# A DiT block in float32: conditioning matmuls placed between two transposes, an elementwise division on another engine, and the last transposes and stores interleaved

## The chip, the cores and the metric

The kernel runs on one core of one Trainium2 chip. The metric is the device time of one launch in microseconds (us). The engines are named as the profile names them: PE (TensorE, matmuls and transposes), PEld (its weight loads), DVE (VectorE), ACT (ScalarE), POOL (GpSimd) and SP (SyncE, which issues most DMAs).

## The reference

Input x is 2 × 2048 × 512 (batch, token, channel), cond is 2 × 512. There are 16 heads of 32 channels; the MLP is 2048 wide.

```python
mod = silu(condition) @ Wada + bada                      # 512 -> 6 x 512
sh_a, sc_a, gt_a, sh_m, sc_m, gt_m = split(mod, 6)
xn = layernorm(x, g1, be1)
xm = xn * (1 + sc_a) + sh_a
x  = x + gt_a * causal_attention(xm, Wqkv, Wproj, bproj)
xn = layernorm(x, g2, be2)
xm = xn * (1 + sc_m) + sh_m
h  = gelu(xm @ W1 + b1)                                  # exact gelu
x  = x + gt_m * (h @ W2 + b2)
```

Everything is float32. In the profile a 128x128 by 128x512 float32 matmul appears as two instructions, so a call of `mm` on such operands counts x2.

## The kernel before

**Stages.** The work goes through the core in this order (times from the trace): startup to about 20 us (first x rows, layer norm statistics, the first two conditioning columns, transposes); q, k and v of batch 0 (to about 215 us), with attention scores woven in between; attention of batch 0 (to 761.8); its projection (`project_phase`, to 820.7); the same for batch 1 (projection 1552.2 to 1611.8); the MLP in four blocks `m` of 1024 tokens, written as a Strassen product with 7 instead of 8 block products (1611.8 to 2415.8); the last block's rows are transposed back and stored (to 2423.1).

**What sets the order.** `mm`, `transpose` and `act` put an instruction into program order on its engine; other DVE, ACT and POOL instructions are placed by a scheduler, which respects data and buffers. DMAs are issued in order by the engine that they are written for (`nc.sync` is SP, `nc.scalar` ACT, `nc.gpsimd` POOL). PSUM has eight banks: six in the pool of the matmuls of the stage (tag `mm`), and two in a pool with tag `s`, which the attention scores (`s`), `ps_mod` and `ps_modt` of the conditioning share; in the MLP these two are a pool of their own for `ps_o`.

**Startup.** `transposed` (L224 on) normalizes x tiles of 128 tokens on DVE (`xn`, L238), transposes them on PE into `ps_xt` (L208) and returns `modulate`, which scales and shifts the four channel chunks into `xmT`, even chunks on DVE (L257), odd ones on ACT (L262). A group of 512 tokens has two halves j = 0, 1 (`norm(g, j)`). `modulation(s0)` computes two of the six column groups: 8 calls of `mm` into `ps_mod` from `w` (the `wada` tile, 2 MB in eight loads), the bias added by DVE (`mr`, L1065), 4 small `mm` that turn rows into columns (`ps_modt`), and a copy (`mod`, L1074). `scale_shift` makes `a` and `c` from them. `picks` makes two constants, `pickc` (4 columns, used by `ps_modt`) and `pick` (L131, 128x512, first used in attention). The order is: stats, both halves' transposes, `picks`, `modulation(0)`, `scale_shift`, both `modulate`, q/k/v.

**q, k and v.** For each of four groups g of 512 tokens, `group` runs products n = 0 to 7 (q and k of four heads each, `ps_qk`) and n = 8 to 11 (v). `among` weaves score matmuls of earlier groups between the matmuls for g > 0; DVE takes each score bank's maxima (`mx`, L455), which frees the bank. After products 5 and 8 the next group's halves are normalized and transposed. After product 3, `modulation(2)` runs in g = 1 and `modulation(3)` in g = 2, the latter followed by `scale_shift`.

**Projection.** `project_phase` takes 16 tiles of 128 tokens, in four chunks k of four tiles. A tile is 4 calls of `mm` into `ps_o`. Attention's outputs arrive undivided: `at` (and at k = 1 a tile that the trace names `kst`) holds 512 tokens × 512 channels of them, `rbs` (the trace's `qst`) the inverse sums spread to the same shape. While chunk k runs, `d` of chunk k + 1 is multiplied by `rbs` (L996), one 128x512 operation for each tile, twelve in a batch. Beside it POOL adds the projection's bias to x for k > 0 (L983), DVE adds x to `ps_o` (L990) and makes the layer norm statistics of the result (L212, L215). For chunk 0 both the division and POOL's addition (L428) are done before the phase. In the first projection, `between` also normalizes and transposes batch 1's first group (n = 5 and 8), and issues the load of Wqkv from POOL at n = 6.

**MLP tail.** For each m, `tail` makes seven products (n = 0 to 6, `ps_y`) with two output chunks each (dd = 0, 1), eight calls of `mm` (f = 0 to 7). Product 6 completes `yt[dd][0]` in `p7`: DVE subtracts (`combine`), ACT scales and shifts (`done`, L1342). `rows_out` transposes `yt` back (PE, `ps_o`, L208), DVE adds the residual (L1410), and SP stores 128 tokens × 512 channels (L1414). In the last m, the rows of group 1 (all four chunks) go ahead of the matmul f = 4 of product 6, dd = 0; chunks 0, 2 and 3 of group 0 go ahead of f = 4 of dd = 1; chunk 1 of group 0 follows after the last product, with the stores of group 0.

Of the kernel before, what the change touches and what calls it, by code (L numbers as in the profile page):

```python
# [17 lines left out]
P = 128  # L18
# [9 lines left out]
def dit_block_kernel(  # L28
# [99 lines left out]
    def picks():  # L128
        two = ident.rearrange("p (k r b) -> p k r b", k=2, r=2)[:, :, :, :B]
        nc.vector.tensor_tensor(pickc, two[:, 0], two[:, 1], ALU.add)  # L130
        nc.vector.tensor_copy(pick, pickc.unsqueeze(3).to_broadcast([P, 2, B, P]))  # L131


    first = const.tile([P, 1], F32, tag="first", name="first")
# [63 lines left out]
    def mm(*args, **kw):  # L198

        return tc.keep_in_program_order(nc.tensor.matmul(*args, **kw))  # L200

    def act(ins):

        return tc.keep_in_program_order(ins)
# [22 lines left out]
    def transposed(pool_, psum, xts, n0, mv, rstd, a, c, b, dst):  # L227

        count = len(xts)
        per = 512 // (count * P)
        xns = []
        for t, xt in enumerate(xts):
            xn = pool_.tile([P, D], F32, tag="xn", name="xn", bufs=3)
            n = n0 + t
            nc.vector.tensor_scalar(  # L238
                xn, xt, mv[:, n, 0:1], rstd[:, n : n + 1], ALU.subtract, ALU.mult
            )  # L240
# [12 lines left out]
        def modulate():  # L253
            for k in range(C):
                src = banks[k // per][:, k % per, :]
                if k % 2 == 0:
                    nc.vector.tensor_scalar(  # L257
                        dst[:, k, :], src,
                        a[:, k, b : b + 1], c[:, k, b : b + 1], ALU.mult, ALU.add,
                    )  # L260
# [679 lines left out]
    def project_phase(row, psum, between):  # L940

        b = row.b
        with pool(f"proj{b}") as pp:
            n = 0
            ats = list(row.at_s)
            rbs = {1: row.rb_s[1], 2: row.old_queries(), 3: row.rb_s[0]}
            rows_x = [b * NT + i * TQ + t for i in last_order for t in range(TQ)]  # L950
            xts = list(row.xt_s)

            def tokens(upto):
                while len(xts) < min(upto, NT):
                    xt = pp.tile([P, D], F32, tag="xt", name="xt", bufs=6)
                    nc.sync.dma_start(xt, x_rows(rows_x[len(xts)]))
                    xts.append(xt)

            row.load_sums(len(units) - 1, len(units))
            tokens(TQ + 6)  # L960
            for k, i in enumerate(last_order):
                if k in (0, 1):

                    at = pp.tile([P, C, QB], F32, tag="at", name="at", bufs=2)
                    nc.sync.dma_start(at, od[b][last_order[k + 2]])
                    ats.append(at)
                at = ats[k]
                for t in range(TQ):

                    if n == 0:  # L970
                        nc.sync.dma_start(rbs[2], wide_d[b][last_order[2]])
                        nc.sync.dma_start(
                            rbs[3][:, : C - 1], wide_d[b][last_order[3]][:, : C - 1]
                        )
                    elif n == 3:
                        row.invert(len(units) - 1, len(units))
                    elif n == 4:
                        row.widen(len(units) - 1, rbs[3][:, C - 1, :])

                    tokens(n + 6)  # L980
                    nt, xt = rows_x[n], xts[n]
                    if k > 0:
                        act(nc.gpsimd.tensor_tensor(xt, xt, bgate, ALU.add))  # L983
                    ps = psum.tile([P, D], F32, tag="mm", name="ps_o")
                    for c in range(C):
                        mm(
                            ps, at[:, c, t * P : (t + 1) * P], row.wproj[:, c, :],
                            start=(c == 0), stop=(c == C - 1),
                        )
                    nc.vector.tensor_tensor(xt, ps, xt, ALU.add)  # L990
                    stats(pp, xt, nt, mv2, True)
                    nc.sync.dma_start(x1d[nt], xt)
                    if k + 1 < NQ:
                        d = ats[k + 1][:, t, :]
                        act(
                            nc.vector.tensor_tensor(d, d, rbs[k + 1][:, t, :], ALU.mult)  # L996
                        )
                    between(n)
                    n += 1
        inv_std(mv2, rstd2, b * NT, (b + 1) * NT)  # L1000
# [3 lines left out]
    with pool("wada") as wp, pool("qkv0") as qp, pool(  # L1004
# [44 lines left out]
        def modulation(s0):  # L1049

            w, mr = wada.pop(s0)
            ps = ps_sp.tile([P, D], F32, tag="s", name="ps_mod")
            for k in range(C // 2):
                for half in range(2):
                    for n in range(2):
                        at = (2 * half + n) * HD
                        kk = half * C // 2 + k  # L1060
                        mm(
                            ps[at : at + HD, :], sc[:, kk, :], w[:, n, kk, :],
                            start=(k == 0), stop=(k == C // 2 - 1),
                        )
            nc.vector.tensor_tensor(mr, ps, mr, ALU.add)  # L1065
            if s0 % 3 == 2:
                return
            ps_t = ps_sp.tile([P, C, 2, B], F32, tag="s", name="ps_modt")
            for k in range(C):
                mm(  # L1070
                    ps_t[:, k], mr[:, k * P : (k + 1) * P], pickc,
                    start=True, stop=True,
                )
            nc.vector.tensor_copy(mod[:, s0 : s0 + 2], ps_t.rearrange("p c s b -> p s c b"))  # L1074

        def scale_shift(a, c, r_g, r_be, shift, scale):

# [7 lines left out]

        for t in range(MTT):
            qkv.stats(0, t)
        halves = [qkv.norm(0, j) for j in range(2)]

        act(  # L1090
            nc.scalar.activation(
# [1 line left out]
            )  # L1093
        )
        picks()
        modulation(0)
        scale_shift(a1, c1, r_g1, r_be1, 0, 1)
        for modulate in halves:
            modulate()

        def also(g, n):

            if g == NG - 1 and n % 2 == 0:
                quarters.step()
            if g == 0 and n == 2:
                load_wada(2, 5)
            elif g == 1 and n == 3:
                modulation(2)
                load_wada(3, 4)
            elif g == 2 and n == 3:  # L1110
                modulation(3)
                scale_shift(a2, c2, r_g2, r_be2, 3, 4)

        quarters = Quarters()
        with pool("hl0") as hp:
# [52 lines left out]
    with ExitStack() as mlp:  # L1168
# [75 lines left out]
        def combine(dst, x, y, op):  # L1244
            nc.vector.tensor_tensor(dst, x, y, op)  # L1245
# [44 lines left out]
        def tail(m, h, yt, w2s, between, among):  # L1290
# [47 lines left out]
                    tiles.append(t)  # L1338
                return lambda f: tiles[f // 2][:, f % 2, :]

            def done(chunk, g):
                nc.scalar.activation(  # L1342
                    yt[chunk][g], yt[chunk][g], AF.Identity,
                    bias=gbias[:, chunk, b : b + 1], scale=gb[:, chunk, b : b + 1],
                )

# [26 lines left out]
                done(HK + dd, 1)  # L1373

            def p7(dd, ps):
                combine(yt[dd][0], us[dd], ps, ALU.subtract)
                done(dd, 0)


            b11, b12, b21, b22 = (0, 0), (1, 0), (0, 1), (1, 1)  # L1380
# [16 lines left out]
                xts.append(xt)  # L1397
            return xts

        def rows_out(m, yt, g, xts, parts, last):  # L1400

            for t in range(MTT):
                ps = ps_op.tile([P, D], F32, tag="o", name="ps_o")
                for lo, hi in parts:
                    for k in range(lo, hi):
# [5 lines left out]
                if last:  # L1411
                    n = (2 * m + g) * MTT + t
                    t0 = (n % NT) * P
                    nc.sync.dma_start(out[n // NT, t0 : t0 + P, :], xts[t])  # L1414

        ready = None
        for m in range(NM):
# [42 lines left out]
            else:  # L1460
# [4 lines left out]

                def among(n, dd, f):

                    if n == 6 and f == HF // 2:
                        if dd == 0:
                            rows_out(m, yt, 1, res[1], [(0, C)], True)  # L1470
                        else:
                            rows_out(m, yt, 0, res[0], [(0, 1), (HK, C)], False)

            tail(m, h, yt, w2s, between, among)
            ready = yt
# [36 lines left out]
```

## Time and profile before

| | us |
|---|---|
| median of 3 runs (lowest, highest) | 2423.33 (2420.83, 2425.81) |
| the profiled execution, its time | 2424.88 |
| its span in the trace | 2423.1 |
| PE busy | 2388.1 (99%) |
| DVE busy | 1358.6 (56%) |
| POOL busy | 1096.5 (45%) |
| ACT busy | 895.1 (37%) |
| mean granted PE clock | 0.997 of full speed |

The profile of one execution was read. Times count from the span's start. A line such as `L996 DVE TENSOR_TENSOR at<-at,qst 128x512 ... x8 | 5.3, 662 | 0.0` says: line 996, engine, operation, output and inputs by their names, shape, number of instructions, busy time in us, mean ns of one, and the idle time of the engine before them, with what ended it. The chain of waits follows the last instruction back to what released it, step by step. The table by stretch gives each engine's busy time in a stretch, the clock that PE was granted (1.00 or 0.50 here), the mean busy share of the DMA engines and their GB/s. Some matmul records are missing from the trace (a block of 8 transposes shows x7).

### The profile page before, as it was taken

Reading aid. Unit: us, or ns where it says so; the run is one execution under the profiler, and the core shown is the slowest. Engines: PE = TensorE matmul, PEld = TensorE weight load, DVE = VectorE, ACT = ScalarE, POOL = GpSimd, SP = SyncE. Lnnn points to the kernel's source line nnn. Section 1 sums busy time; section 2 is a strip of 40 time slices with the busy share of each in tenths; the row PEclk is TensorE's granted clock in tenths of the full one; section 3 lists DMA queues with packets and bytes.
Section 4 is the critical chain, followed back from the end, with each engine's and each line's share of the span. In section 5 each row is a group of like instructions: output and inputs, shape, how many; then the busy total and the mean of one; then the engine's idle time right before and its main releaser. Section 6 shows DMA issues by size and latency. Waiting matters only on the chain.

```text
span 2423.1 us, 31009 instructions
## 1 busy us (share of the span) xinstructions
PE 2388.1 (99%) x10797; PEld 1169.3 (48%) x10797; DVE 1358.6 (56%) x2836; ACT 895.1 (37%) x1670; POOL 1096.5 (45%) x1255
## 2 busy tenths in 40 slices
PE   8999999999999999999999999999999999999998
PEld 3455555555544445555555554444444444444443
DVE  3466666767657536676676765773344263353424
ACT  2213555555554121255555555423213213312310
POOL 1062998978773451199797878322001101100200
PEclk9999999999999999999999999999999999999999
DMA  7677215051325794621515132452324233223323
GB/s 244 195 236 192 53 34 110 23 114 45 105 98 193 216 323 157 158 56 33 120 25 114 45 100 89 166 180 76 110 77 146 76 111 130 80 91 99 114 82 100
DMA packets 132853, 285.72 MB, mean 118 GB/s; under 512 B 13472, under 2 KB 42700, under 8 KB 127832
## 3 DMA queue, kind: packets, MB, share of 16 engines
q1 hardware_dynamic: 126224, 257.46, 35.9%
q0 software_dynamic: 6384, 26.25, 3.1%
q8 instruction: 85, 1.39, 0.2%
q14 instruction: 72, 0.59, 0.1%
q10 hardware_dynamic: 88, 0.02, 0.0%
HBM read 209.76 MB, written 81.79 MB: 120 GB/s over the span
## 4 chain that ended last, share of the span: by engine, by line
PE 95%; DVE 3%; POOL 1%; DMA 1%; issue 1%; ACT 0%; SPq 0%; DVEq 0%; POOLq 0%; ACTq 0%
PE st L200 19%; PE ps_y L200 16%; PE ps_h L200 16%; PE o L200 11%; PE s L200 10%; PE ps_qk L200 8%; PE ps_v L200 4%; PE ps_o L200 4%; PE sm L200 4%; PE ps_xt L208 1%; POOL ee L608 1%; DMA x<-in_x_dram 1%; PE ps_o L208 0%; DVE junk L450 0%; DVE mx L455 0%
## 5 line engine op out<-in xcount | busy, mean ns | idle before, releaser
L580 ACT ACTIVATE e<-st 128x512 f32<-128x512 f32 (+1 forms) x1152 | 573.5, 578 | 427.9 <-PE st L200 363.0
L608 POOL TENSOR_TENSOR ee<-ee,e 128x512 f32<-128x512 f32 x424 | 529.3, 1289 | 4.5 <-ACT e L580 4.2
L455 DVE TENSOR_REDUCE mx<-s 128x1 f32<-128x512 f32 x604 | 407.7, 687 | 205.4 <-PE s L200 204.3
L200 PE MATMUL s<-kst,qst 128*128 128x512 f32 (+3 forms) x1032 | 465.0, 452 | 5.2 <-DVE mx L455 3.2
L200 PE MATMUL st<-qst,kst 128*128 128x512 f32 (+3 forms) x1280 | 409.4, 387 | 0.0
L1283 POOL TENSOR_TENSOR c<-c 128x512 f32<-128x512 f32 x32 | 40.7, 1273 | 625.6 <-DVE c L1245 562.8
L200 PE MATMUL o<-e,vv 128*32 128x512 f32 (+3 forms) x2560 | 300.4, 538 | 2.0 <-POOL e L586 2.0
L200 PE MATMUL ps_h<-sx,w 128*128 128x512 f32 x640 | 286.7, 592 | 0.0
L450 DVE CUSTOM_DVE_ANT_0 junk<-s,causal 128x512 bf16<-128x512 f32 (+3 forms) x428 | 209.1, 488 | 134.0 <-PE s L200 125.7
L200 PE MATMUL ps_y<-sh,w 128*128 128x512 f32 x640 | 278.3, 595 | 0.0
L200 PEld LDWEIGHTS st<-qst,kst 128*128 128x128 f32 x1280 | 227.4, 188 | 94.2 <-issue 62.1
L200 PEld LDWEIGHTS s<-kst,qst 128*128 128x128 f32 x1032 | 194.8, 189 | 155.4 <-DVE mx L455 53.8
L608 POOL TENSOR_TENSOR ee<-e 128x512 f32<-128x512 f32 x168 | 210.4, 1286 | 101.0 <-ACT e L580 100.6
L200 PE MATMUL ps_qk<-xmT,wqkv 128*128 128x512 f32 x512 | 242.8, 602 | 2.2 <-DVE xmT L257 2.2
L1245 DVE TENSOR_TENSOR h<-c,ps_h 128x512 f32<-128x512 f32 x128 | 88.1, 688 | 232.5 <-PE ps_h L200 232.5
L586 POOL TENSOR_SCALAR_AFFINE_SELECT e<-e 128x128 f32<-128x128 f32 (+1 forms) x384 | 122.2, 356 | 200.5 <-ACT e L580 197.8
L200 PEld LDWEIGHTS ps_h<-sx,w 128*128 128x128 f32 x640 | 121.1, 190 | 150.2 <-issue 149.5
L200 PEld LDWEIGHTS ps_y<-sh,w 128*128 128x128 f32 x640 | 121.3, 191 | 148.9 <-issue 147.5
L1269 ACT ACTIVATE h<-h,cols 128x512 f32<-128x512 f32 x128 | 92.4, 722 | 182.0 <-DVE h L1245 182.0
L200 PE MATMUL st<-fold,sel 32*128 32x512 f32 (+1 forms) x1152 | 148.6, 481 | 0.6 <-ACT vv L837 0.2
L200 PEld LDWEIGHTS ps_qk<-xmT,wqkv 128*128 128x128 f32 x512 | 95.4, 193 | 98.9 <-issue 92.1
L200 PEld LDWEIGHTS st<-fold,sel 32*128 32x128 f32 x1152 | 59.1, 181 | 144.3 <-ACT e L580 86.6
(129 smaller groups left out, 2343.2 us busy)
## 6 DMA issues: line engine op xcount, KB each, us to landing
qst<-q SPq DMA_DIRECT2D x128, 256.0 KB
w<-w1d SPq DMA_DIRECT2D x34, 896.0 KB
w<-w2d SPq DMA_DIRECT2D x28, 1024.0 KB
kst<-k SPq DMA_DIRECT2D x24, 1024.0 KB
q<-hl SPq DMA_DIRECT2D x32, 512.0 KB
k<-hl SPq DMA_DIRECT2D x32, 512.0 KB
kst<-k SPq DMA_DIRECT2D x32, 256.0 KB
w<-in_L_cond_W_dram POOLq DMA_DIRECT2D x64, 128.0 KB, 5.3
```

The costliest lines, as they stand in the source:

```text
L200: return tc.keep_in_program_order(nc.tensor.matmul(*args, **kw))
L208: return tc.keep_in_program_order(nc.tensor.transpose(dst, src, ident[:n, :n]))
L450: nc.vector.tensor_tensor_reduce(junk[:, :w], s[:, :w], causal[:, QB - w :], 1.0, MASKED, ALU.add, ALU.max, m,)
L455: nc.vector.tensor_reduce(m, s[:, :w], axis=AX.X, op=ALU.max)
L580: act(nc.scalar.activation(e[:, :w], sts[h][:, :w], AF.Exp))
L586: nc.gpsimd.affine_select(d, d, pattern=[[0, len(tiles)], [1, P]], compare_op=ALU.is_ge, fill=0.0, base=0, channel_multiplier=-1,)
L608: act(engine.tensor_tensor(dst, x, y, ALU.add))
L1245: nc.vector.tensor_tensor(dst, x, y, op)
L1269: nc.scalar.activation(d, d, AF.Gelu, bias=col(r_b1 + chunk, 1))
L1283: nc.gpsimd.tensor_tensor(c1_, c1_, c2_, ALU.subtract)
```

## The change

There are four edits.

1. Startup: the second half's transposes (`norm(0, 1)`) go behind the matmuls of `modulation(0)`. `modulation` now ends with the matmuls into `ps_mod` and returns `columns`, which holds the rest (`mr`, `ps_modt`, `mod`). The `modulate` of both halves goes by pairs of chunks. The copy `pick` goes behind them.
2. Projection: the multiply of L996 is done by GpSimd, in program order (24 instructions in all).
3. `modulation(2)` and `modulation(3)`: the matmuls stay after product 3, `columns` and what follows (the next load of `wada`, or `scale_shift`) go after product 4.
4. Tail of the last m: one token tile of `rows_out` goes ahead of each of f = 4 to 7, where all four went ahead of f = 4. The last product's `combine` and `done` run in two halves of 256 tokens. The last four stores alternate between the queues of SP and ACT.

PE has the same instructions as before, in another order. DVE has 24 multiplies fewer, POOL 24 more; DVE and ACT have one more operation each from the halves.

```diff
@@ picks
         nc.vector.tensor_tensor(pickc, two[:, 0], two[:, 1], ALU.add)
-        nc.vector.tensor_copy(pick, pickc.unsqueeze(3).to_broadcast([P, 2, B, P]))
@@ transposed
-        def modulate():
-            for k in range(C):
+        def modulate(chunks=range(C)):
+            for k in chunks:
@@ project_phase
                         d = ats[k + 1][:, t, :]
                         act(
-                            nc.vector.tensor_tensor(d, d, rbs[k + 1][:, t, :], ALU.mult)
+                            nc.gpsimd.tensor_tensor(d, d, rbs[k + 1][:, t, :], ALU.mult)
                         )
@@ modulation
-            nc.vector.tensor_tensor(mr, ps, mr, ALU.add)
-            if s0 % 3 == 2:
-                return
-            ps_t = ps_sp.tile([P, C, 2, B], F32, tag="s", name="ps_modt")
...
+
+            def columns():
+                nc.vector.tensor_tensor(mr, ps, mr, ALU.add)
+                if s0 % 3 == 2:
+                    return
+                ps_t = ps_sp.tile([P, C, 2, B], F32, tag="s", name="ps_modt")
...
+            return columns
@@ startup
-        halves = [qkv.norm(0, j) for j in range(2)]
+        halves = [qkv.norm(0, 0)]
...
-        modulation(0)
+        columns = modulation(0)
+        halves.append(qkv.norm(0, 1))
+        columns()
         scale_shift(a1, c1, r_g1, r_be1, 0, 1)
-        for modulate in halves:
-            modulate()
+        for k in range(0, C, 2):
+            for modulate in halves:
+                modulate((k, k + 1))
+        act(nc.vector.tensor_copy(pick, pickc.unsqueeze(3).to_broadcast([P, 2, B, P])))
@@ also
-            elif g == 1 and n == 3:
-                modulation(2)
-                load_wada(3, 4)
-            elif g == 2 and n == 3:
-                modulation(3)
-                scale_shift(a2, c2, r_g2, r_be2, 3, 4)
+            elif g in (1, 2) and n == 3:
+                qkv.columns = modulation(g + 1)
+            elif g in (1, 2) and n == 4:
+                qkv.columns()
+                if g == 1:
+                    load_wada(3, 4)
+                else:
+                    scale_shift(a2, c2, r_g2, r_be2, 3, 4)
@@ tail
-            def done(chunk, g):
+            def done(chunk, g, tok=slice(0, MT)):
                 nc.scalar.activation(
-                    yt[chunk][g], yt[chunk][g], AF.Identity,
+                    yt[chunk][g][:, tok], yt[chunk][g][:, tok], AF.Identity,
...
             def p7(dd, ps):
-                combine(yt[dd][0], us[dd], ps, ALU.subtract)
-                done(dd, 0)
+
+                w = MT // 2 if m + 1 == NM and dd + 1 == HK else MT
+                for t0 in range(0, MT, w):
+                    tok = slice(t0, t0 + w)
+                    combine(yt[dd][0][:, tok], us[dd][:, tok], ps[:, tok], ALU.subtract)
+                    done(dd, 0, tok)
@@ rows_out
-        def rows_out(m, yt, g, xts, parts, last):
-
-            for t in range(MTT):
+        def rows_out(m, yt, g, xts, parts, last, tiles=range(MTT)):
+
+            for t in tiles:
...
-                    nc.sync.dma_start(out[n // NT, t0 : t0 + P, :], xts[t])
+
+                    queue = nc.scalar if parts == [(1, HK)] and t % 2 else nc.sync
+                    queue.dma_start(out[n // NT, t0 : t0 + P, :], xts[t])
@@ the last m
-                    if n == 6 and f == HF // 2:
+                    if n == 6 and f >= HF - MTT:
+                        t = [f - (HF - MTT)]
                         if dd == 0:
-                            rows_out(m, yt, 1, res[1], [(0, C)], True)
+                            rows_out(m, yt, 1, res[1], [(0, C)], True, t)
                         else:
-                            rows_out(m, yt, 0, res[0], [(0, 1), (HK, C)], False)
+                            rows_out(m, yt, 0, res[0], [(0, 1), (HK, C)], False, t)
```

More of the change, by code (lines that the diff above doesn't have):

```diff
@@ L1064, in modulation @@
                         )
-            nc.vector.tensor_tensor(mr, ps, mr, ALU.add)
-            if s0 % 3 == 2:
-                return
-            ps_t = ps_sp.tile([P, C, 2, B], F32, tag="s", name="ps_modt")
[L1069 to L1072, printed above, removed]
+            def columns():
[3 more added lines that the diff above has]
+                ps_t = ps_sp.tile([P, C, 2, B], F32, tag="s", name="ps_modt")
+                for k in range(C):
+                    mm(
+                        ps_t[:, k], mr[:, k * P : (k + 1) * P], pickc,
+                        start=True, stop=True,
+                    )
+                nc.vector.tensor_copy(
+                    mod[:, s0 : s0 + 2], ps_t.rearrange("p c s b -> p s c b")
                 )
-            nc.vector.tensor_copy(mod[:, s0 : s0 + 2], ps_t.rearrange("p c s b -> p s c b"))
+            return columns
         def scale_shift(a, c, r_g, r_be, shift, scale):
```

## The prediction

> **What bounds the kernel now.** I read the page first: busy time, then the chain of waits by engine.
>
> ```profile
> PE 2388.1 (99%) x10797; PEld 1169.3 (48%) x10797; DVE 1358.6 (56%) x2836; ACT 895.1 (37%) x1670; POOL 1096.5 (45%) x1255
> PE 95%; DVE 3%; POOL 1%; DMA 1%; issue 1%; ACT 0%; SPq 0%; DVEq 0%; POOLq 0%; ACTq 0%
> ```
>
> TensorE (PE) is the bound, and the change neither adds nor removes a matmul. So it can gain only in two places: the 35 us of the span in which PE is not busy, and PE time spent at half clock, which the page counts as busy. I therefore looked for PE's stalls at the four edited places, first in the chain of waits (start, us, piece), from the startup and from modulation(3):
>
> ```profile
> 7.42 0.33 DVE pick L131
> 12.87 2.73 PE ps_mod L200 x16
> 15.68 0.70 DVE mr L1065
> 18.20 1.46 DVE xmT L257 x3
> ...
> 130.17 0.46 DVE xn L238
> 130.75 0.70 DVE mr L1065
> 131.49 1.05 PE ps_modt L200 x8
> ```
>
> PE stands still from 130.17 to 131.49 (xn, 0.12 of issue, mr). Next, PE's timeline in the last product, and the groups of the first projection (761 to 822 us; busy time, mean ns of one, idle before and its releaser):
>
> ```profile
> 2407.88 0.55 PE L208 MATMUL ps_o<-ident,yt 128*128 128x128 f32 x3 [0.60 <-DVE x L1410]
> 2410.46 5.29 PE L200 MATMUL ps_y<-sh,w 128*128 128x512 f32 x8
> 2417.38 0.44 PE L208 MATMUL ps_o<-ident,yt 128*128 128x128 f32 x2 [1.63 <-ACT yt L1342]
> ```
> ```profile
> L200 PE MATMUL ps_o<-kst 128*128 128x512 f32 x64 | 28.2, 596 | 1.6 <-DVE kst L996 1.6
> ...
> L983 POOL TENSOR_TENSOR xt<-xt,bgate 128x512 f32<-128x512 f32 x12 | 15.6, 1313 | 35.7 <-DMA xt<-in_x_dram 27.1 <-DVE kst L996 6.2 <-DVE at L996 2.4
> ...
> L996 DVE TENSOR_TENSOR kst<-kst,qst 128x512 f32<-128x512 f32 x4 | 5.3, 1336 | 0.0
> L996 DVE TENSOR_TENSOR at<-at,qst 128x512 f32<-128x512 f32 x8 | 5.3, 662 | 0.0
> ```
>
> Last, the table by stretch (PE, PEld, DVE, ACT, POOL busy; granted clock; DMA share; GB/s), cut in 3.4 us pieces:
>
> ```profile
> 17.80:21.20 3.40, 1.50 (x2) 0.83 (x3) 2.23 (x7) 1.93 (x4) 1.29 (x3) 0.50 1.06 388
> 130.40:133.80 3.40, 2.45 (x16) 1.68 (x13) 1.69 (x7) 0.00 (x0) 2.85 (x4) 1.00 1.08 225
> 133.80:137.20 3.40, 3.40 (x7) 1.61 (x6) 0.80 (x3) 0.00 (x0) 1.47 (x3) 0.50 1.03 361
> 2407.10:2410.50 3.40, 1.58 (x11) 0.94 (x10) 1.86 (x6) 0.00 (x0) 0.00 (x0) 1.00 0.02 8
> 2410.50:2413.90 3.40, 3.40 (x7) 1.32 (x6) 0.42 (x1) 0.00 (x0) 0.00 (x0) 0.50 0.00 0
> 2413.90:2417.30 3.40, 1.86 (x5) 0.55 (x3) 0.69 (x1) 0.78 (x1) 0.00 (x0) 1.00 0.00 0
> ```
>
> A piece in which PE idled is followed by one at clock 0.50: after the startup chain, after the stall at 130, and after the tail's run of transposes. Each costs time later, under matmuls that look busy.
>
> **The clock, by rule and by row.** The Trainium skill, "TensorE: Matmul & The Clock Gate", "Why this matters for your kernels", asks only for no gap above some 3 us between bursts. By it, a 1.3 us stall costs 1.3 us. The rows say more: the piece 130.40 to 133.80 held a 1.09 us rest of the stall and eight tiny matmuls (ps_modt), and the next ran at 0.50. There the pairs of ps_qk take 1.44 and 1.71 us in the chain instead of 0.86; with the score instructions between them that is some 1.73 us more. The same page's Part 4 says that transposes do not count as PE work in the same way; the piece at 2407.10, transposes alone, agrees (next piece 0.50), and the one at 2413.90, 54% matmul, was followed by no loss. I use the rows.
>
> **Edit 1, startup.** The pick copy (0.33) leaves the DVE chain ahead of the first rstd (recip, 7.75); I take 0.25 of it as saved. The second half's seven-record transpose block (11.12 to 12.87) goes behind ps_mod, but ps_mod cannot use that: wada's eight 256 KB loads land from 7.78 to 13.80, and its last matmuls need the last of them, so it ends at 15.2 (matmuls warm) to 16.0 (cold) instead of 15.47. Queued behind it on PE now are eight transposes, and behind these ps_modt, which the whole chain waits for. At the full clock, which 14.4 to 17.8 had (1.00), they take 8 × 0.11 = 0.9 us and fit into the wait for mr (0.8): 0. The first product now waits for two xmT operations of DVE and not three: −0.49. Sum −0.75. At half clock (0.21 each) they would overrun mr: +0.2 to +0.8. The first products' half clock (2.45 us, 19.7 to 24.6) may stay (0) or be avoided (−2.45); PE is less idle, but transposes are what fills it, as at 2407, so 0. The pick copy waits behind the modulates and only delays later DVE work by 0.33, unneeded until attention. Neither step issues a DMA. I take **−0.7**, ends −3.2 and +0.1.
>
> **Edit 3, modulation(2) and (3).** The mr add and ps_modt go one product (3.45 us) later, so xn 0.46 + issue 0.12 + mr 0.70 + 0.04 = 1.32 us of stall is covered by four q/k matmuls and the scores between them. New waits: ps_mod keeps one of the two banks that scores use for a product longer, so scores run on one bank. The score behind waits for its bank's mx (0.69 us, the page's mean); putting the rows in the new order, bank by bank, leaves about 0.25 us at ps_modt (0 to 0.8). Behind the waiting mr on DVE stand mx reductions of the scores, as before. With no stall in the piece the clock stays: −1.73. If ps_modt's eight tiny matmuls (1.05) lower it by themselves, that part is 0. modulation(2), at 79.7, had no stall and gets none: the same bank shift, 0 to +0.3. wada's next load and scale_shift move one product later with slack of tens of us: 0. Sum −1.32 −1.73 +0.25 = **−2.8**, ends −3.1 and −0.8.
>
> **Edit 2, division on GpSimd.** Only the first projection stalls: PE stands 1.59 us before 779.87 for the last kst multiply. That multiply took 2.48, another 1.53, while POOL ran the xt additions; alone they take 0.67. Here a rule speaks against the edit: "GPSIMD Engine Reference", section 4.1, "Engine selection", wants two-input elementwise work on VectorE, GpSimd taking about twice as long. Rows: 1.27 (POOL's add) against 0.66, so 12 × 0.61 = 7.3 us more engine time per batch. But the row that PE waits for is 2.48, not 0.66. By the rule alone the stall grows by 0.6; by the rows POOL is free at 761.6 (its last earlier operation ends there) and the four multiplies end at 761.6 + 4 × 1.3 = 766.8, where PE needs them at 775.5. After that POOL alternates addition and multiply, 2.55 a tile, against 3.43 + PE's extras (14.6 us per four tiles, 10.3 used): ready about 786.5 for 790, and 801.2 for 804.7, slack 3.5 each. wqkv's three issues (3 × 0.77), queued in the same order, come about 4 us later; they feed products 40 us away. What waits behind a POOL multiply is the next xt addition, for which DVE's L990 waits, and then the PSUM bank; six banks cover that. DVE loses 10.6 us of work. One new collision: xn beside a POOL operation took 1.49 (at 1585.04) against 0.54, so the transposes at n = 5 and 8 may wait 0 to 0.7. I take 0.5: −1.6 + 0.5 = **−1.1** (0 to −1.6). The second projection had no stall: 0.
>
> **Edit 4, tail.** For dd = 0 the 16 transposes took 2.47 with DVE waits; spread between matmuls they cost their own 1.75: −0.72. For dd = 1 the block took 2406.07 to 2410.46 = 4.39; with a matmul ahead of each tile, one tile costs 0.11 + 0.38 wait + 0.38 = 0.875 (the wait stays, the additions use the same bank): 3.5, so −0.89. The half clock after it costs 5.15 for 3.43 us of ps_y, 1.72. Interleaved, ps_y fills 0.86 of 1.735 us, 50%, nearer the piece with 54% that kept its clock than the pure transposes that lost it: −1.72, other end 0. From the last matmul to the first x addition is 2.28 now (DVE 0.69, ACT 0.81, transposes); in halves about 1.73: −0.55. The second queue for two of four stores: the stores land 0.67 apart with the DMA engines full, so 0. Sum **−3.9** (−2.2 to −3.9).
>
> **Sum** −0.7 −2.8 −1.1 −3.9 = −8.5. From the profiled execution (2424.88, span 2423.1) 2416.4; from the median 2414.8. The profile lies 1.55 above the median, so I take the middle, 2415.6.
>
> **Rivals.** (A, 0.62) All four as above: 2412.5 to 2418.5. (B, 0.20) The clock drops anyway, since transposes and tiny matmuls fill the pieces: +0.8 −1.1 −1.1 −2.2 = −3.6, 2419.7 to 2421.3. For it: the pieces at 17.8 and 2410.5; against: the one at 2413.9. (C, 0.09) The stalls only change their names, score banks at modulation(3) and wada's last load at the start: −0.5 to −2, 2421 to 2424. (D, 0.06, slower) GpSimd as one queue in the projections: it decides when addition plus multiply exceed 14.6 / 4 = 3.65 us. The rows give 2.55; if its two SBUF reads met DVE's each time and both doubled, as L996's did, a tile takes 5.1, POOL falls 5.9 behind at each of two boundaries per batch, 23.5 in all, less slack 7: +16, with the other edits −7.4, 2432 to 2434. Against it: L983 keeps 1.31 even in the densest stretch. (E, 0.03) The startup's clock is saved too: below 2412.5.
>
> **How the numbers follow.** This kernel's measurement can tell 0.2% (4.85 us) from no change: faster means below 2418.5. That is A and E less A's upper edge (0.01): 0.64. B, C and that edge lie within: 0.30. D is slower: 0.06. The range, 2412.0 to 2421.5, holds A and B, 0.82; it leaves out most of C, D and most of E.
>
> **What will show it.** Edit 1: the first ps_qk starts at 18.9 to 19.2, not 19.70. Edit 3: the eight ps_modt come without an idle PE and the piece after is at 1.00; a wait for mx before them speaks for C. Edit 2: no PE wait at 779; POOL's multiplies at about 1.27, and PE not waiting for POOL at 790 and 804; if it does, D. Edit 4: four groups of transposes with ps_y between them, clock 1.00 until the last product, and 1.7 us from its end to the first addition. A new PE wait at another place would make the prediction wrong, above all in the score stream around the two modulations or in the second projection.

## The result and the profile after

The changed kernel takes 2413.47 us (median of 6 runs, 2412.25 to 2415.88) against 2423.02 before (6 runs): ratio 0.996, 95% interval 0.995 to 0.997. That is 9.55 us less, where 7.7 were predicted (2415.6). The profiled execution took 2412.76, its span is 2411.0. (Line numbers of the changed kernel differ a little: its L199 is L200 of the kernel before.)

The page's busy times and the chain of waits by engine:

```profile
PE 2381.4 (99%) x10797; PEld 1167.1 (48%) x10797; DVE 1345.9 (56%) x2813; ACT 896.4 (37%) x1671; POOL 1125.3 (47%) x1279
...
PE 96%; DVE 2%; POOL 1%; issue 0%; DMA 0%; ACT 0%; SPq 0%; DVEq 0%; POOLq 0%; ACTq 0%
```

PE's busy time fell by 6.7 us with the same number of instructions: that fits the half clock that is gone (13.7 us up to the last product's end in the profile before, none here; half of 13.7 is 6.8). The rest is idle time, 35.0 before and 29.6 now.

**Startup**, chain of waits (start, us, piece):

```profile
11.16 3.44 PE ps_mod L199 x16
14.59 1.02 PE ps_xt L207 x8
15.62 0.88 PE ps_modt L199 x8
...
17.21 1.01 DVE xmT L256 x2
...
18.26 7.13 PE ps_qk L199 x16
```

The second half's transposes (ps_xt at 14.59) lie where PE waited for mr, and two xmT operations instead of three precede the first ps_qk, which starts at 18.26 instead of 19.70. The table by stretch, after, for the startup, modulation(3) and the tail:

```profile
14.40:17.80 3.40, 2.09 (x17) 1.83 (x16) 1.86 (x7) 0.00 (x0) 0.96 (x2) 1.00 1.06 395
17.80:21.20 3.40, 2.94 (x7) 1.43 (x8) 1.64 (x4) 1.93 (x4) 0.59 (x2) 1.00 1.05 386
130.40:133.80 3.40, 3.40 (x16) 2.18 (x15) 2.17 (x9) 0.60 (x1) 1.01 (x2) 1.00 1.06 302
133.80:137.20 3.40, 3.40 (x16) 2.18 (x16) 2.41 (x6) 0.60 (x1) 1.65 (x3) 1.00 1.03 390
2394.70:2398.10 3.40, 3.01 (x10) 1.30 (x9) 0.64 (x2) 0.23 (x1) 0.00 (x0) 1.00 0.60 230
2398.10:2401.50 3.40, 2.63 (x11) 1.11 (x10) 1.25 (x5) 0.00 (x0) 0.00 (x0) 1.00 0.00 0
```

The third column from the right, the granted clock, is 1.00 at all three places that showed 0.50 before.

**Projection**, groups of the first one, first xn before (761 to 822 us), then the changed kernel (750 to 815 us) with the longest xn as a single row:

```profile
L238 DVE TENSOR_SCALAR xn<-qst,mv,rstd 128x512 f32<-128x512 f32 x4 | 2.0, 540 | 0.0
```
```profile
L199 PE MATMUL ps_o<-kst 128*128 128x512 f32 x64 | 27.9, 594 | 0.0
```
```profile
L237 DVE TENSOR_SCALAR xn<-qst,mv,rstd 128x512 f32<-128x512 f32 x4 | 8.3, 2096 | 0.0
```
```profile
779.56 4.88 DVE L237 TENSOR_SCALAR xn<-qst,mv,rstd 128x512 f32<-128x512 f32 x1
```
```profile
L995 POOL TENSOR_TENSOR at<-at,qst 128x512 f32<-128x512 f32 x8 | 10.6, 1322 | 6.8 <-DMA x1d<-kst 6.8
L995 POOL TENSOR_TENSOR kst<-kst,qst 128x512 f32<-128x512 f32 x4 | 4.9, 1268 | 0.0
```

PE's 1.6 us stall is gone. GpSimd's multiplies cost 1.27 to 1.32 us on average. The collision moved to xn, 2.10 us on average where it was 0.54. The average hides four unequal operations: 0.54, 1.40, 1.57 and 4.88 us, the last beside four GpSimd operations in a row. PE did not wait for it here.

**Tail**, PE's timeline:

```profile
2397.28 0.44 PE L207 MATMUL ps_o<-ident,yt 128*128 128x128 f32 x2 [0.39 <-DVE x L1426]
...
2405.10 0.44 PE L207 MATMUL ps_o<-ident,yt 128*128 128x128 f32 x2 [1.15 <-ACT yt L1354]
```

One 0.39 us wait stays in each tile, as forecast, and the wait for the last yt is 1.15 instead of 1.63.

To see where time went, the starts of the same DVE and ACT instructions in two traces are subtracted (medians over 20 us). From before to after this gives −3.85 us once the first products have run, −2.7 at modulation(3), −1.7 at the first projection, −0.4 scattered, −3.4 in the tail: −12.1, the difference of the two profiled executions (2424.88 and 2412.76). The medians differ by 9.55 only. So a profile is one sample, and the experiments had to say what is typical.

### The profile page after: what moved, and what is told of

Same layout as the page of the kernel before. It is cut to its first block, busy times and chain, and to the rows that moved or that the text cites. A ratio compares the mean times of both kernels' runs of the same rounds, so it can differ in the third digit from the quotient of the medians.

```text
span 2411.0 us, 31023 instructions
## 1 busy us (share of the span) xinstructions
PE 2381.4 (99%) x10797; PEld 1167.1 (48%) x10797; DVE 1345.9 (56%) x2813; ACT 896.4 (37%) x1671; POOL 1125.3 (47%) x1279
## 4 chain that ended last, share of the span: by engine, by line
PE 96%; DVE 2%; POOL 1%; issue 0%; DMA 0%; ACT 0%; SPq 0%; DVEq 0%; POOLq 0%; ACTq 0%
PE st L199 19%; PE ps_h L199 16%; PE ps_y L199 16%; PE o L199 11%; PE s L199 10%; PE ps_qk L199 9%; PE ps_o L199 5%; PE ps_v L199 4%; PE sm L199 4%; PE ps_xt L207 1%; POOL ee L607 1%; PE ps_o L207 1%; DMA x<-in_x_dram 0%; DVE junk L449 0%; DVE mx L454 0%
## 5 line engine op out<-in xcount | busy, mean ns | idle before, releaser
L199 PE MATMUL s<-kst,qst 128*128 128x512 f32 (+3 forms) x1032 | 463.8, 451 | 4.7 <-DVE mx L454 2.9
L199 PE MATMUL st<-qst,kst 128*128 128x512 f32 (+3 forms) x1280 | 409.2, 387 | 0.0
L199 PE MATMUL o<-e,vv 128*32 128x512 f32 (+3 forms) x2560 | 300.6, 538 | 2.0 <-POOL e L585 2.0
L199 PE MATMUL ps_h<-sx,w 128*128 128x512 f32 x640 | 286.7, 592 | 0.0
L199 PE MATMUL ps_y<-sh,w 128*128 128x512 f32 x640 | 277.6, 592 | 0.0
L199 PEld LDWEIGHTS st<-qst,kst 128*128 128x128 f32 x1280 | 227.4, 188 | 94.2 <-issue 62.1
L199 PEld LDWEIGHTS s<-kst,qst 128*128 128x128 f32 x1032 | 194.4, 189 | 154.4 <-DVE mx L454 55.2
L199 PE MATMUL ps_qk<-xmT,wqkv 128*128 128x512 f32 x512 | 239.0, 594 | 1.8 <-DVE xmT L256 1.8
L199 PEld LDWEIGHTS ps_h<-sx,w 128*128 128x128 f32 x640 | 121.1, 190 | 150.2 <-issue 149.7
L199 PEld LDWEIGHTS ps_y<-sh,w 128*128 128x128 f32 x640 | 120.3, 190 | 144.9 <-issue 143.5
L199 PE MATMUL st<-fold,sel 32*128 32x512 f32 (+1 forms) x1152 | 148.6, 481 | 0.6 <-ACT vv L836 0.2
L199 PEld LDWEIGHTS ps_qk<-xmT,wqkv 128*128 128x128 f32 x512 | 93.9, 190 | 96.9 <-issue 90.4
L199 PEld LDWEIGHTS st<-fold,sel 32*128 32x128 f32 x1152 | 59.1, 181 | 144.2 <-ACT e L579 86.6
```

## The experiments

Times are medians; "before" ran beside each set of runs (2423.54, 2424.13, 2423.55 and 2423.53).

The changed kernel itself was not run again beside the later sets, and the medians of "before" differ by up to 1.1 us between sets. So a difference of about 1 us between two versions from different sets is not shown by their medians alone.

**Each edit alone** (numbered as in the section on the change; each kernel is the kernel before plus that edit's part of the diff).

> The kernel before with the startup edit alone. Theory (the half clock behind the startup is avoided because the second half's transposes fill PE's wait): the first ps_qk starts near 18.3 us instead of 19.70 and the first products run at clock 1.00, so -3.9 us in a profile against that of before, and -1.5 to -3.9 at the median. Rival, as the prediction had it (only the chain gets shorter, the clock part stays): -0.7 to -1.4 us, and the profile shows 0.50 for some 3.4 us behind the first ps_qk.

2420.29, ratio 0.9984 (0.9975 to 0.9992): −3.3 us (−6.1 to −1.9). Its profile has the first ps_qk at 18.72 and no half clock behind it. Both fit the theory; how often the clock is saved is seen below.

> The kernel before with only the multiply of the projection moved from VectorE to GpSimd. Theory (VectorE's multiply lost time only where it met GpSimd's additions): PE's 1.59 us stall before 779.87 goes and no new one comes, -1.6 to -1.8 us. Rival (xn beside GpSimd takes 2 us instead of 0.5 and the transposes wait for it): -0.5 to -1.1. Rival that GpSimd as a queue falls behind: +1 or more, with PE waits near 790 and 804.

2420.27, ratio 0.9986 (0.9977 to 0.9995): −3.3 us (−5.6 to −1.2). The stall is gone; instead PE waits 0.63 us for xn, as the second theory had it. Its trace, aligned, saves 1.2 at the place; the median gains more than either expectation, and where the rest comes from is not shown.

> The kernel before with only modulation(2) and modulation(3) split, their columns one product later. Theory: the stall at 130.17 (1.32 us) and the half clock behind it (1.7 us) both go, -2.7 us, the piece behind ps_modt at clock 1.00. Rival (eight tiny matmuls lower the clock by themselves): -1.0 to -1.3 us, and a piece at 0.50 behind ps_modt.

2423.53, ratio 0.9999 (0.9990 to 1.0007): no difference, though its trace, aligned, saves 2.7 us at the place. Neither expectation holds at the median.

> The kernel before with the tail edit alone (transposes by token tile, last product in halves, two store queues). Theory: -3.4 us: 0.7 from each block's waits, 1.7 from the clock that stays at 1.00, 0.5 from the halves, nothing from the queue. Rival (the pieces with half transposes lose the clock too): -1.7 to -2.2, with a piece at 0.50 in the last 10 us.

2421.09, ratio 0.9990 (0.9981 to 0.9999): −2.5 us (−4.6 to −0.2), the tail at 1.00 up to the last matmul. Between the two expectations.

The four medians add up to −9.0 us, near the whole change's 9.55, but each has an interval of some 2 us to either side, so this does not show that the edits leave each other alone. The next runs ask the changed kernel which parts carry the gain.

**Where edit 3 went.**

```diff
             elif g in (1, 2) and n == 3:
-                qkv.columns = modulation(g + 1)
-            elif g in (1, 2) and n == 4:
-                qkv.columns()
+                modulation(g + 1)()
                 if g == 1:
```

> The changed kernel with modulation(2) and modulation(3) whole again after product 3 (edit 3 undone). With edit 3 alone the median did not move (-0.0), though its profile saved the stall and the half clock behind it. Theory (the stall of 1.3 us is always paid by the old order, the half clock behind it in most executions but not in all): 2.0 to 3.0 us above the changed kernel's 2413.5, so about 2416, and the stall back before ps_modt. Rival (the split order pays as much elsewhere, by its clock or its score banks): 0 to 0.5 above it.

2413.91 (5 runs, 2413.43 to 2417.07): 0.4 above the changed kernel, as the rival had it. The traces show how. From ps_mod to the next ps_xt the changed kernel takes 11.29 us (124.76 to 136.05), the undone one 12.31 (128.79 to 141.10): undoing costs 1.02 us there, about PE's wait for mr (0.95, and 0 with the split). Then 0.74 comes back at the start of attention, near 212 us. There the changed kernel's chain shows a wait that the undone one does not have:

```profile
212.87 0.59 ACT vv L836
...
213.51 0.93 PE st L199 x3
```

The first attention matmuls (st) wait for ACT's copy of the last v product, most likely since one of them takes over its PSUM bank (the trace names the wait, not the bank). In the undone kernel, as with edit 1 alone, the same st run without a stop; in the kernel before and with edit 3 alone they wait. So edit 1 alone gains this 0.75 us as well, and with edit 3 beside it the gain is lost again. An edit 80 us earlier changes which st has to wait; why is not shown. The same was undone in the fastest version (below):

> The version with filling and transposes together (2410.8), with modulation(2) and modulation(3) whole again, as a second look at edit 3 with less spread from the startup. Theory (the old order pays 0.75 us at modulation(3), which comes back at the start of attention, where the split order waits for v's last copy and the old one does not; on top of it the half clock behind the stall, in about half of the executions): 0.3 to 1.5 us above 2410.8, the aligned traces +0.75 at 132 us and -0.75 near 212. Rival (the split saves the whole stall and clock): 2.0 to 3.0 above. Rival (the split order gives nothing at all): 0 or below.

2411.83 (2409.91 to 2412.31) against 2410.77 (2410.02 to 2413.28), +1.1; the aligned traces give +1.01 at modulation(3), of which 0.25 is back 8 us later, and −0.73 at 212. The stall that comes back later is confirmed. That edit 3 beyond this keeps the half clock of some executions is not shown: the spreads overlap, the profile of this run lost no clock at modulation(3), and its five executions were granted 0.999 to 1.000, as the five with edit 3 were.

**What in edit 1 saves the clock.**

```diff
-        halves = [qkv.norm(0, 0)]
+        halves = [qkv.norm(0, j) for j in range(2)]
...
-        columns = modulation(0)
-        halves.append(qkv.norm(0, 1))
-        columns()
+        modulation(0)()
```

> The changed kernel with both halves' transposes ahead of modulation(0) again; the later pick copy and the modulates by pairs of chunks stay. Theory (the second half's transposes in the wait for mr keep PE busy enough for the clock): the first ps_qk at 18.7 to 19.2 us, then 0.50 for a piece or two, so 2.5 to 3 us above 2413.5. Rival (the shorter DVE chain, pick and pairs, is what does it): within 0.5 us of 2413.5, the startup at 1.00.

2416.0 (8 runs, 2414.11 to 2420.45): +2.5, the theory's size, with the first ps_qk at 19.43, later than the 18.7 to 19.2 expected. The granted clock behind it:

```profile
17.80:21.20 3.40, 1.77 (x2) 0.84 (x3) 2.71 (x9) 1.93 (x4) 1.47 (x3) 0.51 1.06 388
21.20:24.60 3.40, 3.40 (x5) 1.35 (x4) 0.69 (x1) 0.00 (x0) 0.00 (x0) 0.50 0.86 314
```

Filling PE's remaining wait tests the same from the other side. The version also takes the tail's wait out (see the last experiment); the figure without the filling is from there:

```diff
                 nc.vector.tensor_copy(
                     mod[:, s0 : s0 + 2], ps_t.rearrange("p c s b -> p s c b")
                 )
+                if s0 == 0:
+                    ps_f = ps_sp.tile([P, D], F32, tag="s", name="ps_f")
+                    for k in range(2):
+                        mm(ps_f, ident, w[:, 0, k, :], start=(k == 0), stop=(k == 1))
```

> The changed kernel with the transposes of a token tile ahead of both additions, and with two further matmuls of 128x512 (into a spare bank that nobody reads) behind ps_modt in the startup, where PE waits for xmT. Theory (the half clock behind the startup, seen in 2 of 5 profiles of kernels with the startup edit, follows from PE's idle time before the first ps_qk): the startup is at 1.00 in the profile, the median 1 us below that of the same kernel without the filling (2412.3), so about 2411.3. Rival (the half clock is decided by the earlier wait for wada's loads, inside ps_mod): no change at the median, and pieces at 0.50 behind the first ps_qk as often as without; the filling itself may delay ps_qk by up to 0.3.

2410.77 (2410.02 to 2413.28) against 2412.32 without the filling. In the chain the fill stands between ps_modt and the first ps_qk, and the clock is whole:

```profile
15.88 1.82 PE ps_f L199 x4
17.70 12.67 PE ps_qk L199 x29
```
```profile
17.80:21.20 3.40, 3.40 (x9) 1.48 (x10) 1.03 (x3) 1.37 (x4) 0.00 (x0) 1.00 1.05 385
```

The medians differ by 1.55 with 5 runs each, from different sets. The granted clocks speak more clearly: 0.999 to 1.000 in all five executions with the filling, 0.998 to 0.999 in the five without. The profile alone would not decide it, since ps_mod ended early in it (13.98). Useless matmuls pay here, and the clock is the likely reason. (This kernel's profile, 2413.28, lies high because of a stall with a half clock behind it at 867 us, in batch 1's first group, which no edit touches.)

**How often the clock is lost.** Every kernel left one profile. Counted over all of them, with and without the edit that bears on the place (a piece with a clock under 0.95 in which the next useful matmuls run; the cost is that of the first profile that showed it, and at the startup others paid 1.7 to 3.1; the projection's new order is counted without the kernel that has extra GpSimd work):

| place | cost | old order | new order |
|---|---|---|---|
| startup | 2.45 | 5 of 5 | 3 of 7; with the filling 0 of 2 |
| modulation(3) | 1.7 | 3 of 6 | 0 of 8 |
| first projection | 1.7 | 1 of 5 | 0 of 8 |
| tail | 1.72 | 2 of 4 | 0 of 10 |

With the new order the startup lost the clock where ps_mod, which waits for wada's loads, ended late: at 15.16, 15.19 and 15.59 in the three that lost it, at 14.25 to 15.05 in the four that did not. The counts are small, and no single row of the table is proof.

The traces show one reason why the same code can lose the clock or keep it. Within each trace all half-clock stretches start whole multiples of 3.413 us apart (in the profile before at 17.77, 133.82 and 2410.51: 34 and 667 of them). So it matters how a stall falls on this raster. In the tail of before and of edit 3 alone, one raster piece held most of the transposes (PE 47 and 48% busy), and the next was at half clock. With edits 1 and 2 alone the same transposes fell on two pieces (65 and 71% busy), and the clock stayed. The busy share alone is not the rule: at modulation(3), pieces of 72% were followed by half clock in three profiles and by none in two.

The record also has the mean granted clock of every execution, profiled or not. What an execution lost is (1 − clock) × span. The clock is given to three decimals, a step of 2.4 us, so averages are used; and the half clock after the last product, which hardly costs time, is in the figure for every kernel.

| kernel | executions | mean clock | lost to the clock, us | mean time less that, us |
|---|---|---|---|---|
| before (beside the single edits) | 33 | 0.9976 | 5.8 | 2417.6 |
| edit 1 alone | 11 | 0.9984 | 4.0 | 2415.7 |
| edit 2 alone | 11 | 0.9978 | 5.3 | 2415.2 |
| edit 3 alone | 11 | 0.9975 | 6.2 | 2416.7 |
| edit 4 alone | 11 | 0.9977 | 5.5 | 2415.6 |
| changed kernel | 6 | 0.9993 | 1.6 | 2412.0 |

The differences to before have standard errors of 0.5 to 0.7 us in the clock's column and 0.3 to 0.5 in the last. So the change as a whole won 4.2 us of clock and some 5.6 us elsewhere. Of the single edits only the first wins clock beyond the noise (1.8). Edits 3 and 4 alone win none that shows (+0.4 and −0.3), in spite of their rows in the table of counts; their gain (0.8 and 2.0) lies outside the clock. Edit 1's 1.9 outside the clock fits its earlier first ps_qk (18.6 on average in seven profiles, 19.6 in the four with the startup of before) and the 0.75 at the attention's start. Edit 2's 2.4 is more than its stall (1.6 to 1.9).

**Edit 2 undone in the changed kernel** (L995 on VectorE again):

> The changed kernel with the projection's multiply on VectorE again (edit 2 undone). Alone, the edit gave -3.3 us at the median (interval -1.2 to -5.6), its profile shows -1.3 to -1.7 in the first projection and nothing in the second. Theory (only the stall before the fourth tile's multiply goes): 1.4 to 1.8 us above the changed kernel's 2413.5, so about 2415.1, PE waiting some 1.5 us on the kst multiply. Rival (something beyond the stall is gained too, a half clock or the second projection): 2.5 to 3.5 us above, with a PE wait or a piece at 0.50 at another place of the projections.

2415.72 (7 runs, 2414.22 to 2418.76), +2.25: between theory and rival, and the profile shows why. PE's wait, and the stretches with and behind it:

```profile
774.13 6.21 PE L199 MATMUL ps_o<-kst 128*128 128x512 f32 x10 [1.91 <-DVE kst L995]
```
```profile
771.90:775.30 3.40, 1.49 (x3) 0.65 (x3) 2.90 (x7) 0.30 (x1) 0.27 (x1) 0.82 1.03 430
775.30:778.70 3.40, 3.40 (x7) 1.43 (x6) 2.35 (x6) 0.00 (x0) 0.00 (x0) 0.68 1.02 402
```

Here the stall was followed by a half clock, and the traces differ by 4.6 us at the projection; in the four other profiles with the old multiply (1.59 to 1.77 us of wait) it was not. One VectorE multiply took 3.66 us in this profile, beside the end of GpSimd's issues of the wqkv loads and the first two of three xt additions:

```profile
767.38 3.66 DVE L995 TENSOR_TENSOR kst<-kst,qst 128x512 f32<-128x512 f32 x1
```
```profile
765.68 2.29 POOL L772 DMA_DIRECT2D wqkv<-in_L_cond_Wqkv_dram  x3
767.98 4.18 POOL L982 TENSOR_TENSOR xt<-xt,bgate 128x512 f32<-128x512 f32 x3
```

The Trainium skill, "SBUF — State Buffer", "SBUF: two separate sides", says that a VectorE operation with two SBUF inputs and a GpSimd operation that reads SBUF exclude each other on a shared port pair, the loser waiting a whole instruction. The rows agree for the multiply (0.67 alone; 1.53, 2.48 and 3.66 beside GpSimd), and in the other direction for the additions (1.27 alone, 1.65 and 1.73 where a multiply was running as they started). The multiply began 0.6 us before the first addition, when GpSimd was only issuing a DMA, and did not get through; whether it waited for the issue is open. An xn of the changed kernel took 1.57 us (0.54 alone) from 775.89, with nothing but such issues on GpSimd; a multiply of the profile before ran to its end beside one (at 772.03, the issue from 771.41).

**Case D brought about.**

```diff
                             nc.gpsimd.tensor_tensor(d, d, rbs[k + 1][:, t, :], ALU.mult)
                         )
+                        for _ in range(2):
+                            spare = pp.tile([P, D], F32, tag="spare", name="spare")
+                            act(
+                                nc.gpsimd.tensor_tensor(
+                                    spare, d, rbs[k + 1][:, t, :], ALU.mult
+                                )
+                            )
```

> The changed kernel with two further GpSimd multiplies of the same size beside each of L995's (written to a spare tile that nobody reads), so that a tile costs GpSimd 3 x 1.27 = 3.8 us for k = 0 and 4 x 1.27 = 5.1 us after it, against 3.65 us of matmuls. This is the prediction's case D, made on purpose. Theory (GpSimd is one queue and decides from 3.65 us a tile): PE waits for multiplies or additions near the starts of k = 2 and 3 in the first projection and k = 1 to 3 in the second, 8 to 16 us slower than the changed kernel. Rival (the slack of the tiles ahead, six x tiles and six banks, covers it): under 3 us slower.

2437.52, ratio 1.006 to before, +24 us to the changed kernel, more than the 8 to 16 expected. PE waits for GpSimd at the chunks' starts:

```profile
794.01 1.66 PE L199 MATMUL ps_o<-kst,at 128*128 128x512 f32 x2 [4.80 <-POOL at L995]
...
814.59 13.12 PE L199 MATMUL ps_o<-kst,at 128*128 128x512 f32 x26 [4.00 <-POOL at L995]
```

The mechanism is the one feared, and above 3.65 us a tile it costs more than the +16 worked out: the aligned traces lose 13 us in the first projection and 10 in the second. Half-clock stretches from 794.46, 814.94 and 1610.25, together 13.7 us, are part of it. At 2.55 us a tile nothing of it appears.

**The last product and the store queues** (`w = MT` and `queue = nc.sync` in the changed kernel):

> The changed kernel with the last product's subtraction and scaling in one piece and the last four stores on one queue. Theory: from the last matmul to the first x addition 2.0 us instead of 1.5, and the stores as far apart as with two queues, +0.5 us, about 2414. Rival (the second queue also shortens the last landings): +1 or more, with the last landing 0.5 us or more later after the first addition.

2413.72, +0.25. From the last matmul's end to the end of the first x addition 2.28 us (2403.97 to 2406.25) against 1.81 (2403.96 to 2405.77): the halves give 0.47 there. The end of the span follows the first addition by 5.05 us with one queue and 5.23 with two: the second queue gives nothing, and of the 0.47 only 0.2 is left at the end. (Halves and queue were undone together, so their shares at the end are not separated.)

**The tail's wait.**

```diff
                 for lo, hi in parts:
                     for k in range(lo, hi):
                         transpose(...)
+                for lo, hi in parts:
                     d = slice(lo * P, hi * P)
                     nc.vector.tensor_tensor(xts[t][:, d], ps[:, d], xts[t][:, d], ALU.add)
```

> The changed kernel with all transposes of a token tile ahead of its additions, where chunk 0's addition stood between them in the last block. Theory (the four 0.38 us waits on DVE, at 2396.9, 2398.7, 2400.5 and 2402.3 us, come from the addition on the same bank): -1.5 us, about 2412, and no PE wait inside the tiles. Rival (PE then waits for ps_o's two banks instead): -0.5 or less, with waits on x's addition before the tiles.

2412.32 (2411.23 to 2414.12), −1.15. No PE wait is left inside the tiles; a tile with its matmuls takes 1.19 us in place of 1.79, and the aligned traces gain 2.4 us in the tail, more than the 1.5 of the waits alone. That fits the theory; the median moved by less, in 5 runs from another set. With the filling this is the fastest version, 2410.77 (ratio 0.9947 to before, 0.9934 to 0.9961).

## Why the prediction was right, by its steps

The sum was right (−8.5 by the working, 9.55 measured, within the range), and the places were the right ones. But two terms came out too small and two too large, so that the sum came so near is in good part luck.

| step | forecast | alone | undone in the changed kernel |
|---|---|---|---|
| 1 startup | −0.7 | −3.3 | +2.5 (the transposes' place) |
| 2 division | −1.1 | −3.3 | +2.25 |
| 3 columns | −2.8 | 0.0 | +0.4 and +1.1 |
| 4 tail | −3.9 | −2.5 | +0.25 (halves and queue only) |

1. **Startup: too small.** The chain's part was right in kind (two xmT operations take 1.01 us where three took 1.46: 0.45, forecast 0.49), and ps_mod did end where forecast or earlier (14.25 to 15.6 in seven profiles). The failed term is "transposes are what fills it, so 0" for the 2.45 us of half clock. The old order lost it in 5 of 5 profiles, the new one in 3 of 7, and all executions with edit 1 alone win 1.8 us of clock on average. This is the mechanism of the small case E (0.03), and it is frequent, though the median stayed above E's 2412.5.
2. **Division: too small.** One row was misread: the last kst multiply, which PE waited for, took 0.66 us. The 1.53 and the 2.48 belong to the two before it, which made it late; the chain before shows it (it counts 2.40 of the 2.48, from the end of the instruction ahead).

```profile
774.38 2.40 DVE kst L996
...
779.24 0.59 DVE kst L996
```

The conclusion holds, since these slow multiplies are what set the time, and GpSimd's factor of two cost nothing. The failed term is the 0.5 us taken off for xn (PE waited 0 to 0.63 for it), and the stall varies: 1.59 to 1.91 us, once with a half clock behind it. The interval of the single edit, −5.6 to −1.2, nearly includes the forecast, and part of the median's gain stays unexplained.
3. **Columns: too large.** The mechanism stands (no wait ahead of ps_modt, 1.00 behind it), but both sizes failed. The 1.32 us piece of the chain was 0.95 us of PE idle, and undoing the edit costs 1.0. The half clock behind it, counted in full at 1.73, occurs in 3 of 6 profiles, and the executions with edit 3 alone show no clock won. And 0.75 us is paid back by a wait for ACT's copy 80 us later, which the step said nothing of.
4. **Tail: a little too large.** The blocks (0.93 us a tile against 0.875) and the queue (0) were close; the halves gave 0.47 against 0.55 at the first addition, of which 0.2 reached the end. The guess from the 54% piece was right: 0 of 10 profiles lost the clock. The failed term is 1.72 for a half clock that the old order has in 2 of 4 profiles; outside the clock edit 4 alone won 2.0 us, the forecast without that term being 2.2.

So the errors of 1 and 2 (some −4.8 us) and of 3 and 4 (some +4.2) cancel. The common one: each clock term was taken as the one profile showed it, all or nothing, where it is a matter of frequency. The clock was forecast to be won at edits 3 and 4 (3.45 us) and not at 1; the executions show it won at 1. Of the rivals, B (the clock drops anyway) fell for the change as a whole, which loses 1.6 us to the clock where the kernel before loses 5.8. D's mechanism is real, but was seen only with 1.5 to 2 times the GpSimd work a tile. C's idea, a stall that changes its place, holds for part of edit 3, though at the start of attention and not at the score banks.

## What to carry to other kernels

Where a profile shows PE at half clock behind a short stall, look at several executions, or at several kernels with that part unchanged, before the loss is counted in full; the mean granted clock of each execution, where it is at hand, says more than a count over few profiles. A stall of PE ahead of real matmuls can be worth filling, even with useless ones, as at this startup. A slow engine may be right for an operation if the fast one is slow there: read the row that the bound engine waits for, with the rows ahead of it in time, and not the mean. And judge an edit by aligned traces beyond its place, because a saved wait can come back at a later stage.

## What the runs showed of the hardware that was not expected

- Stalls of 1 to 2 us were enough to halve PE's clock in the next 3.4 us, in some executions and not in others of the same code (modulation(3): 3 of 6 profiles); the half-clock stretches of a trace lie on a raster of 3.413 us.
- Over 65 executions of the kernel before, the granted clock goes with the time: 2424.8 us on average at 0.997 (41 of them), 2422.2 at 0.998 (12), 2420.8 at 0.999 (11).
- A VectorE multiply with two SBUF inputs took 3.66 us beside GpSimd's additions (0.67 alone), and xn, a VectorE operation that reads one tile, went from 0.54 to as much as 4.88 us beside GpSimd, while the addition with a PSUM input (L990 before) kept 0.69.
- Two store queues for four 256 KB stores gained nothing over one (5.23 and 5.05 us from the first addition to the end).
